# Layer 3's attention product by seven half-block products in a four-layer graph network on Trainium2

## The chip, the cores and the metric

The kernel runs on one core of one Trainium2 chip. The time is the device time in microseconds (us) of one execution, and the median over several executions is given. The core's engines are TensorE (PE in the profile, with PEld for its weight loads), VectorE (DVE), ScalarE (ACT), GpSimd (POOL) and the queue of SyncE (SP), which issues most DMAs.

## The reference

The input is 32 independent graphs of 512 nodes with 256 fp32 features each (`x`), and an integer adjacency matrix per graph (`adj`). Four attention layers follow one another, each with a layer norm and a ReLU ahead of it and a residual sum behind it. Layer 3, cut to what matters:

```
h   = relu(layernorm(x))
k   = h @ W
e   = leaky_relu((k @ a_1)^T + k @ a_2 + (k @ a_12) @ k^T)
e   = where(adj > 0, e, -9e15)
out = x + elu(h @ W_1 + (softmax(e) @ h) @ W_2)
```

## The kernel before

**Tiling.** A graph's 512 nodes are four tiles of 128 partitions (`NT` = 4); its 256 features are two halves of 128 (`HC` = 2, `HALF` = 128). Everything is fp32 on TensorE. A graph is a list of some hundred operations, made by `graph(b, ...)`, for each of `B` = 32 graphs. In each layer: layer norm (`normed`: statistics L558 on VectorE, the power L564 on GpSimd, the offset L567 on VectorE, the scaling L571 on ScalarE), a transposition by DMA (L576, L579, L591), values `v` = h times a weight (`scored_values`, matmuls at L809), scores, mask, exponential, the attention product (`attend`, L758), and the layer's end.

**Products by halves.** A product of two 2x2 block matrices takes eight block products, or seven if sums of blocks are formed ahead (Strassen's scheme in Winograd's form). The helper `seven` (L617) does the latter: the seven block products are written one after the other into two PSUM banks, `p` and `q`; between them ScalarE or VectorE copies or adds a result out (`write`, `add`), so that each product can accumulate onto what stands in the bank. The kernel before uses it for the features (L783), the values and `w3` (L809) and the scores (L874, L1042). `block_sums` (L649) forms the sums on VectorE. The attention product itself, in all four layers, is the plain one.

**Layer 3.** The scores come out transposed, keys on partitions, into two buffers `e3_0` and `e3_1` of two key tiles each. VectorE adds mask and bias (L1049, L1057), the row maximum is found by way of `crest3` (L1066 to L1085, two DMA transpositions), VectorE subtracts it (L1091), ScalarE takes the exponential of each buffer (L1094). `v3` holds h times W_2 in two halves of 128 columns, each with one more column; the last columns of a row are set to one, which lets the product give the sum of a row's weights. `w3` is h times W_1 less one. `attend(3, ...)` then multiplies: for two groups of two query tiles, for each of four key tiles, two matmuls of a 128x128 block of `e` with 259 columns of `v3`, into one bank for each query tile. The end of the layer, `fourth`, reads the bank: VectorE takes the reciprocal of the sum (L1123) and forms y = bank x reciprocal + `w3` (L1128). L1134, L1137 and L1140 form the elu and the residual, and a DMA on GpSimd's queue stores the graph (L1157).

**The order of work.** The class `Plan` orders the operations of all graphs. Each has an engine, a cost pair (how long it holds its engine, and when its result is there), operations that it comes after, and the buffers that it uses. `Plan.order` walks through a modelled time: on each engine the ready operation with the earliest due time goes next, if its buffers are free. Due times come from the last operation backward, with a spacing between graphs; `Plan.best` tries 64 pairs of spacings and keeps the order whose replay ends first. Each engine then executes its instructions in that order. Six graphs can be in flight (`FLIGHT`); the large buffers are 34 pages of 4 KB per partition (`PAGES`), PSUM has 8 banks, and there are 5 buffers for `v`.

Of the kernel before, what the change touches and what calls it, by code (L numbers as in the profile page):

```python
# [11 lines left out]
F32 = mybir.dt.float32  # L12
# [4 lines left out]
ALU = mybir.AluOpType  # L17
PSUM = bass.MemoryType.PSUM

P = 128  # L20
# [13 lines left out]
def pe(n512=0, n258=0, n256=0, nt=0):  # L34
    t = n512 * PE512 + n258 * PE258 + n256 * PE256 + nt * PET
    return t, t + 170.0
# [3 lines left out]
V_MASK, V_CODE, V_HALF, V_PSUM, V_ADD = (602.0, 683.0), (600.0, 690.0), (600.0, 690.0), (395.0, 484.0), (334.0, 425.0)  # L40
A_COPY, A_HALF, A_PRELU, A_EXP, A_TANH = (477.0, 597.0), (253.0, 373.0), (570.0, 693.0), (519.0, 640.0), (373.0, 474.0)
A_BIAS, A_PRELU2 = (570.0, 687.0), (629.0, 722.0)
G_POW, G_STORE = (800.0, 850.0), (900.0, 900.0)
V_SUM, V_BLOCK, V_FULL = (334.0, 425.0), (790.0, 880.0), (1140.0, 1225.0)
A_EXP_TWO, A_PRELU_TWO = (960.0, 1070.0), (1050.0, 1160.0)
A_HALF_BIAS = (345.0, 460.0)
# [161 lines left out]
def kernel(  # L208
# [31 lines left out]
    nc = tc.nc  # L240
    B, N, H = x.shape
    NT = N // P
    HC = H // P
    HALF = H // 2
# [4 lines left out]
    LEAD = 2  # L249

    const = ctx.enter_context(tc.tile_pool(name="const", bufs=1))
    work = ctx.enter_context(tc.tile_pool(name="work", bufs=1))
# [4 lines left out]
    cols, pair, stat, turned = [P, HC, N], [P, NT, H], [P, NT], [P, NT, N]  # L257
# [4 lines left out]
        "hT": (cols, F32, "page"), "fa": (cols, F32, "page"), "zT": (cols, F32, "page"), "row": (cols, F32, "page"),  # L262
        "xn": (pair, F32, "page"), "y": (pair, F32, "page"), "z": (pair, F32, "page"), "r": (pair, F32, "page"),
        "w": (pair, F32, "page"), "crest": ([P, 4, N], BF16, "page"),
        "hs": ([P, 4, N // 2], F32, "page"), "fs": ([P, 4, N // 2], F32, "page"),
        "code": (turned, BF16, "code"), "adj": (turned, I32, "adj"),
        "planes": ([P, 2, H], U16, "planes"), "planesT": ([P, 2 * HC, P], U16, "planesT"),
# [158 lines left out]
    for n, dst, w, key in (("w0", w0_s, w0, "raw9"), ("att", att_s, att_w, "raw10")):  # L426
# [11 lines left out]
    a = [load(l1_sb, rows_of(l1_w), "raw0")]  # L438
    t = transposed(l1_sb, lambda: halves(l1_wide()), a, "raw0", "raw11")
# [4 lines left out]
    a = [load(lambda i=i: halves(l2_wide())[:, :, i, :], rows_of(l2_w)[:, :, i * HALF : (i + 1) * HALF], "raw12")  # L444
         for i in range(2)]
    t = transposed(lambda: halves(l2_wide()), l2_wt, a, "raw1", "raw12")
    a = t + [load_column(l2_ac, l2_a.rearrange("o n -> (o n)"))]
    a = a + product(lambda d: l2_wide()[:, d, :: HALF + 1], l2_wt,
                    lambda c: l2_ac.rearrange("p (o c) -> p c o", o=2)[:, c, :], 2, a, "raw1", "raw12")
    ready["l2"] = seven_of(l2_wide, l2_aug, HALF + 1, a, "raw12")  # L450

    t = transposed(l3_sb, wt3, [load(l3_sb, rows_of(l3_w), "raw2")], "raw2", "raw4")
    a = product(lambda d: awt()[:, d, :], a12_sb, lambda c: wt3()[:, c, :], H,
                t + [load(a12_sb, rows_of(l3_a12), "raw3")], "raw3", "raw4", "raw5")
    a = product(lambda d: m3_sb()[:, d, :], wt3, lambda c: awt()[:, c, :], H, a, "raw4", "raw5", "raw6")
# [4 lines left out]
    a = [load(lambda i=i: l3_wide()[:, :, i * (HALF + 1) : i * (HALF + 1) + HALF],  # L460
              rows_of(l3_w2)[:, :, i * HALF : (i + 1) * HALF], "raw8") for i in range(2)]
# [8 lines left out]
    for i in range(VALUES):  # L470
        v = const.tile([P, NT, LEAD + H + 1], F32, tag=f"v{i}", name=f"v{i}")
# [4 lines left out]
    def graph(b, adj_before, x_before):  # L476


        T = Tiles(b)

        def op(engine, cost, after, emit, *keys, size=0, weights=()):
            return plan.op(engine, cost, after, emit, b, T.uses(keys) + W.uses(weights), size)

        def two(g):
            return slice(2 * g, 2 * g + 2)

        def half(i):
            return slice(i * N // 2, (i + 1) * N // 2)
# [45 lines left out]
        for g in range(NT // 2):  # L534
            code = op("V", V_CODE, [got_adj[2 * g + 2], code], partial(classes, g), "adj", "code", "slot")
            for t in (2 * g, 2 * g + 1):
                if b:
                    coded.append(op("D", D_TURN, [code], partial(turn_code, t), "code", "codeT"))
                else:
                    key = f"bank_c{t}"  # L540
                    a = op("PE", pe(nt=NT), [code], partial(turn_code_pe, t, key), "code", key)
# [75 lines left out]
        def seven(key, cost, after, keys, work, write, add, beside=0):  # L617

            p, q = f"bank_{key}p", f"bank_{key}{'p' if beside else 'q'}"

            def times(x, bank, start, fresh, *wait):
                return op("PE", cost, after(x) + list(wait), lambda: work(x, T[bank][:, start:], fresh), bank, *keys)

            c11 = write(0, 0, p, 0, [times(1, p, 0, True)])
            two = times(2, q, beside, not beside, c11)
            c12 = write(0, 1, p, 0, [times(6, p, 0, False, c11)])
            c22 = write(1, 1, p, 0, [times(7, p, 0, False, c12)])  # L640
            four = times(4, p, 0, False, c22)
            c21 = write(1, 0, p, 0, [four])
            c11 = add(0, 0, q, beside, [two, c11])

            c22 = add(1, 1, q, beside, [times(5, q, beside, True, four, c11), c22])
            c12 = add(0, 1, q, beside, [times(3, q, beside, False, c22), c12])
            return {(0, 0): c11, (0, 1): c12, (1, 0): c21, (1, 1): c22}
# [100 lines left out]
        def attend(l, es, vs, use):  # L748


            done, a = [], None
            lead = (LEAD, 1, 1, 0)[l]
            for ts in parts(l):
                keys = [f"bank_a{l}{t}" for t in ts]

                def product(ts, c, keys):
                    for t, key in zip(ts, keys):
                        nc.tensor.matmul(T[key][:, : LEAD + H + 1 - lead], e(l, c)[:, t * P : (t + 1) * P],  # L758
                                         T[f"v{l}"][:, c, lead:], start=(c == 0), stop=(c == NT - 1))

                for c in range(NT):
                    a = op("PE", pe(n258=2 * len(ts)), [es[c], vs[c], a], partial(product, ts, c, keys),
                           *keys, f"v{l}", f"e{l}_{c // 2}")
                done += [use(t, a, key) for t, key in zip(ts, keys)]
            return done

        def product_of(key):

# [45 lines left out]
        if b == 0:  # L814

            qs, vs, es = [], [], []
            for k in range(HC):
                key = f"bank_f0{k}"
# [6 lines left out]
                a = op("PE", pe(n512=4), hs + ready["raw10"], partial(features, k, key), key, "hT0", weights=["raw10"])  # L825
                qs.append(op("A", A_COPY, [a], lambda k=k, key=key: nc.scalar.copy(T["fa0"][:, k, :], T[key]), key, "fa0"))
            for t in range(NT):
                key = f"bank_v0{t}"
# [6 lines left out]
                a = op("PE", pe(n256=4), [hs[t]] + ready["raw9"], partial(values, t, key), key, "hT0", weights=["raw9"])  # L835
                vs.append(op("V", V_ADD, [a], lambda t=t, key=key: nc.vector.tensor_add(
                    T["v0"][:, t, LEAD : LEAD + H], T[key][:, :H], b0_sb), key, "v0"))
            for c in range(NT):
                key = f"bank_q0{c}"

                def similar(c, key):
# [4 lines left out]
                a = op("PE", pe(n512=4), qs, partial(similar, c, key), key, "hT0", "fa0")  # L846
                a = op("A", A_COPY, [a], lambda c=c, key=key: nc.scalar.activation(
                    e(0, c), T[key], AF.Exp, scale=float(H) ** -0.5), key, f"e0_{c // 2}")
                es.append(op("V", V_MASK, [a, m0], lambda c=c: nc.vector.tensor_tensor(
                    e(0, c), e(0, c), T["mask0"][:, c, :], ALU.mult), "mask0", f"e0_{c // 2}"))  # L850
        else:
            right_after, right = block_sums("hs0", "hT0", lambda j, l, T=T: T["hT0"][:, j, half(l)], hs, left=False)
# [10 lines left out]
            def add_v0(i, l, key, start, after):  # L863
# [3 lines left out]
            vs = seven("v0", pe(nt=4), lambda x, after=right_after: after(x) + ready["w0"], ("hT0", "hs0"),  # L867
                       partial(by_nodes, w0_s, right), write_v0, add_v0, beside=N // 2)
            vs = [tuple(vs.values())] * NT
            left_after, left = block_sums("fs0", "fa0", lambda i, j: T["fa0"][:, j, half(i)], qs, left=True)  # L870
# [27 lines left out]
            es = {}  # L898
# [3 lines left out]
            es = [(es[0, c // 2], es[1, c // 2]) for c in range(NT)]  # L902
# [21 lines left out]
        a = None  # L924
        for c in range(NT):
            a = op("PE", pe(n512=4), [ys[c], a], partial(again, c), "bank_z0", "bank_z1", "y0", f"e0_{c // 2}")
        zs = [op("A", A_COPY, [a], partial(evacuate_z, k), f"bank_z{k}", "zT") for k in range(HC)]
        xs = []
        for g in range(NT // 2):
            key = f"bank_o{g}"  # L930
# [18 lines left out]
            a = op("PE", pe(n256=8), zs + ready["w1"], partial(second_conv, g, key), key, "zT")  # L949
            bs = [op("V", V_PSUM, [a] + ready["b1"], partial(biased, 2 * g + j, key), key, "z0") for j in range(2)]  # L950
            a = op("A", A_EXP, bs, partial(tanh2, g), "z0")
# [7 lines left out]
        right_after, right = block_sums("hs1", "hT1", lambda j, l: T["hT1"][:, j, half(l)], hs, left=False)  # L959
        vb = scored_values(1, right_after, right, l1_aug, ready["l1"])  # L960
        vs = [tuple(vb.values())] * NT
        es = leaky_exp_t(1, vs, 1.0)
        es = [op("V", V_FULL, [es[g]], partial(masked1, g), "codeT", f"e1_{g}") for g in (0, 1)]
        es = [es[c // 2] for c in range(NT)]
# [16 lines left out]
        right_after, right = block_sums("hs2", "hT2", lambda j, l: T["hT2"][:, j, half(l)], hs, left=False)  # L981
        vb = scored_values(2, right_after, right, l2_aug, ready["l2"])
        vs = [tuple(vb.values())] * NT
        es = leaky_exp_t(2, vs, -1.0)
# [4 lines left out]
        es = [op("V", V_FULL, [es[g]], partial(masked2, g), "codeT", f"e2_{g}") for g in (0, 1)]  # L989
        es = [es[c // 2] for c in range(NT)]  # L990
# [26 lines left out]
        us, xs = attend(2, es, vs, third), []  # L1017
        for g in range(NT // 2):
            a = op("V", V_MASK, [u[0] for u in us[two(g)]], partial(add_lower, g), "y2", "x")
# [122 lines left out]
        def store_part(ts):  # L1142
            nc.sync.dma_start(out=out[b].rearrange("(t p) h -> p t h", p=P)[:, ts, :], in_=T["y3"][:, ts, :])

        us = attend(3, es, vs, fourth)
        last = []
        for ts in parts(3):
            ts = slice(ts[0], ts[-1] + 1)
# [55 lines left out]
```

## Time and profile before

| what | value |
|---|---|
| median of 3 executions | 2356.08 us (2354.88 to 2357.17) |
| profiled execution | 2353.99 us |
| its span, first to last instruction | 2351.9 us |
| granted TensorE clock | 1.00 |
| PE, PEld busy | 2327.6, 1991.7 us |
| DVE, ACT, POOL busy | 2000.2, 1687.7, 263.5 us |

The span is the profiled execution seen from its first instruction to its last; the 2.1 us beside it are start and end. Busy time is the time in which an engine has at least one instruction under way. A matmul's shown duration overlaps with the next one's, so what a matmul costs is read from start to start. Each fp32 matmul of the source stands in the profile as two MATMUL records, each with a weight load of its own.

### The profile page before, as it was taken

The numbers are of one execution on the slowest core, as the hardware profiler recorded it, in microseconds if no ns is written. First come the engines' busy times: TensorE is split into PE (matmuls) and PEld (weight loads), VectorE is DVE, ScalarE is ACT, GpSimd is POOL, SyncE is SP. The second block draws the span as 40 slices with busy tenths as digits, with TensorE's granted clock in tenths as the row PEclk, the third lists the DMA queues.
The fourth block names the chain that finished last, engine by engine and source line by source line (L and its number), as shares of the span: only waits on it lengthen the run. The fifth ranks groups of instructions, "written<-read, shape, count | busy, mean of one in ns | idle before, by whom it ended". The sixth has DMA issues, their size and how long they took to land.

```text
span 2351.9 us, 36467 instructions
## 1 busy us (share of the span) xinstructions
PE 2327.6 (99%) x12374; PEld 1991.7 (85%) x12374; DVE 2000.2 (85%) x5100; ACT 1687.7 (72%) x3165; POOL 263.5 (11%) x316
## 2 busy tenths in 40 slices
PE   7999999999999999999999999999999999999998
PEld 5888888888888898888888888988888888888887
DVE  6878788888888898888988888988889888887898
ACT  5567677767787767786767876777867677766884
POOL 3000111010111110110111111101111011010110
PEclk9999999999999999999999999999999999999999
DMA  7431233422333423334323343323342333421321
GB/s 197 90 77 39 52 84 77 92 61 73 92 68 86 91 49 86 79 75 94 84 55 83 73 86 72 90 62 70 88 93 57 78 92 62 90 55 25 59 52 41
DMA packets 429850, 178.18 MB, mean 76 GB/s; under 512 B 384128, under 2 KB 401664, under 8 KB 429664
## 3 DMA queue, kind: packets, MB, share of 16 engines
q1 hardware_dynamic: 424288, 157.51, 31.3%
q0 software_dynamic: 5232, 18.23, 2.4%
q8 instruction: 97, 1.59, 0.3%
q14 instruction: 89, 0.73, 0.1%
q10 hardware_dynamic: 144, 0.13, 0.0%
HBM read 67.64 MB, written 16.89 MB: 36 GB/s over the span
## 4 chain that ended last, share of the span: by engine, by line
PE 94%; DVE 3%; ACT 2%; DMA 1%; issue 0%; SPq 0%; DVEq 0%; ACTq 0%
PE bank_a L758 36%; PE bank_z L918 9%; PE bank_o L936 5%; PE bank_s3p L1042 5%; PE bank_q0p L874 4%; PE bank_f3p L783 4%; PE bank_v0p L809 4%; PE bank_f0p L783 4%; PE bank_w3p L809 4%; PE bank_q0q L874 3%; PE bank_s3q L1042 3%; PE bank_v1p L809 2%; PE bank_v2p L809 2%; PE bank_v3p L809 2%; PE bank_v1q L809 2%; PE bank_v3q L809 2%
## 5 line engine op out<-in xcount | busy, mean ns | idle before, releaser
L758 PE MATMUL bank_a<-v,e 128*128 128x258 f32 (+2 forms) x4096 | 1027.2, 381 | 3.0 <-DVE e L956 2.2
L758 PEld LDWEIGHTS bank_a<-v,e 128*128 128x128 f32 x4096 | 736.3, 190 | 108.9 <-issue 23.2
L591 ACT COPY hT<-planesT 128x512 uint16<-128x512 uint16 x508 | 383.2, 768 | 182.1 <-DMA planesT<-planes 170.7
L564 POOL TENSOR_TENSOR rstd<-ve,mhalf 128x2 f32<-128x2 f32 x256 | 227.9, 899 | 1896.9 <-DVE ve L561 1684.2
L571 ACT ACTIVATE xn<-x,off,rstd 128x256 f32<-128x256 f32 x512 | 284.8, 597 | 115.5 <-DVE off L567 115.2
L918 PE MATMUL bank_z<-e,y 128*128 128x512 f32 x512 | 240.8, 592 | 0.6 <-ACT y L909 0.6
L576 DVE COPY planes<-xn 128x512 uint16<-128x512 uint16 x380 | 155.9, 419 | 41.1 <-DMA planesT<-planes 28.3
L558 DVE BATCH_NORM_STATS2 st<-x 128x6 f32<-128x512 f32 x256 | 175.7, 695 | 5.0 <-DMA x<-in_x_dram 4.8
L732 ACT ACTIVATE e<-row,v 128x512 f32<-128x512 f32 x224 | 153.9, 721 | 0.0
L918 PEld LDWEIGHTS bank_z<-e,y 128*128 128x128 f32 x512 | 92.8, 190 | 66.2 <-issue 59.8
L735 ACT ACTIVATE e<-e 128x1024 f32<-128x1024 f32 x128 | 135.9, 1062 | 0.1
L936 PE MATMUL bank_o<-w_sb,zT 128*128 128x256 f32 x512 | 120.3, 379 | 0.0
L1049 DVE SCALAR_TENSOR_TENSOR e<-bank_s3p,v,mask 128x256 f32<-128x256 f32 x256 | 111.4, 476 | 10.2 <-PE bank_s3p L1042 9.1
L936 PEld LDWEIGHTS bank_o<-w_sb,zT 128*128 128x128 f32 x512 | 96.9, 190 | 13.0
L667 DVE TENSOR_TENSOR hs<-hT 128x512 f32<-128x512 f32 x127 | 86.7, 683 | 24.2 <-ACT hT L591 24.1
L664 DVE TENSOR_TENSOR hs<-hT,hs 128x256 f32<-128x256 f32 x254 | 105.8, 417 | 1.5
L1091 DVE TENSOR_TENSOR e<-e,crest 128x1024 f32<-128x1024 f32 x64 | 78.0, 1220 | 32.3 <-ACT crest L1085 32.3
L956 DVE SCALAR_TENSOR_TENSOR e<-codeT,e 128x1024 f32<-128x1024 bf16 x64 | 78.1, 1220 | 30.8 <-ACT e L735 30.6
L885 DVE TENSOR_TENSOR e<-bank_q0p,mask 128x512 f32<-128x512 f32 x124 | 84.7, 683 | 16.5 <-PE bank_q0p L874 15.9
L882 ACT ACTIVATE e<-e 128x512 f32<-128x512 f32 x124 | 77.9, 630 | 28.6 <-DVE e L893 25.0
L940 DVE SCALAR_TENSOR_TENSOR z<-bank_o,rs,b_sb 128x256 f32<-128x256 f32 x128 | 56.9, 479 | 41.1 <-PE bank_o L936 40.4
L695 ACT COPY v<-bank_v2p 128x258 f32<-128x258 f32 x128 | 47.9, 374 | 58.2 <-PE bank_v2p L809 57.4
(201 smaller groups left out, 4799.8 us busy)
## 6 DMA issues: line engine op xcount, KB each, us to landing
adj<-in_adj_dram SPq DMA_DIRECT2D x128, 256.0 KB
x<-in_x_dram SPq DMA_DIRECT2D x31, 512.0 KB
out_dram<-y POOLq DMA_DIRECT2D x31, 512.0 KB, 3.7
row<-row SPq DMA_DIRECT2D x56, 256.0 KB
planesT<-planes SPq DMA_TRANSPOSE x508
codeT<-code SPq DMA_TRANSPOSE x124
crest<-crest SPq DMA_TRANSPOSE x64
row<-sT SPq DMA_DIRECT2D x56, 2.0 KB
```

The costliest lines, as they stand in the source:

```text
L558: nc.vector.bn_stats(T[f"st{l}"][:, g, :], T["x"][:, two(g), :].rearrange("p t h -> p h t"))
L564: nc.gpsimd.tensor_tensor(T[f"rstd{l}"][:, two(g)], T[f"ve{l}"][:, two(g)], mhalf[:, two(g)], ALU.pow)
L571: nc.scalar.activation(T[f"xn{l}"][:, t, :], T["x"][:, t, :], AF.Relu, bias=T[f"off{l}"][:, t : t + 1], scale=T[f"rstd{l}"][:, t : t + 1])
L576: (nc.scalar.copy if l in BYACT else nc.vector.tensor_copy)(T[f"planes{l}_{t}"], bits)
L591: nc.scalar.copy(bits[:, :, :, t * P : (t + 1) * P], T[f"planesT{l}_{t}"].rearrange("p (b c) n -> p b c n", b=2))
L758: nc.tensor.matmul(T[key][:, : LEAD + H + 1 - lead], e(l, c)[:, t * P : (t + 1) * P], T[f"v{l}"][:, c, lead:], start=(c == 0), stop=(c == ...
L783: nc.tensor.matmul(p[:, : N // 2], w[:, x - 1, :], right(x), start=fresh, stop=True, skip_group_check=True)
L809: nc.tensor.matmul(p[:, j * k : (j + 1) * k], right(x)[:, j * P : (j + 1) * P], w[:, x - 1, :], start=fresh and j == 0, stop=True, skip_gr ...
L874: nc.tensor.matmul(p[:, j * N // 2 : (j + 1) * N // 2], right(x)[:, j * P : (j + 1) * P], left(x), start=fresh and j == 0, stop=True, skip ...
L918: nc.tensor.matmul(T[f"bank_z{k}"], T["y0"][:, c, k * P : (k + 1) * P], e(0, c), start=(c == 0), stop=(c == NT - 1))
L936: nc.tensor.matmul(T[key][:, j * H : (j + 1) * H], T["zT"][:, k, t * P : (t + 1) * P], w1_sb[:, k, :], start=(k == 0), stop=(k == HC - 1))
L1042: nc.tensor.matmul(p[:, j * N // 2 : (j + 1) * N // 2], left(x)[:, j * P : (j + 1) * P], right(x), start=fresh and j == 0, stop=True, skip ...
```

## The change

For graphs 0 to 26, layer 3's attention product is done by `seven`; the last five graphs keep `attend`. The new function `attend_by_seven` forms four sums of blocks of `v3` (`one_and_three`, which makes two at once, `two_` and `four_`) and four sums of blocks of the weights `e` (`weights_one` to `weights_four`) on VectorE. Three of these stand in new pages (`es3_0`, `es3_1`, `vs3`), `two_` and `weights_two` overwrite blocks of `v3` and `e3_0`. One GpSimd memset (`edge`) writes the columns that carry row sums in one of the sums. Each of the seven products is four matmuls of a 128x128 block with 128 columns, or 130 in products 3 and 5. ScalarE copies four results from PSUM to `y3` and VectorE adds three onto it; two of the adds come with a reciprocal of two columns. `both_terms_of` then forms y from `y3` in SBUF where `both_terms` read PSUM. `seven` itself now takes its list of buffers for each product.

```diff
+V_SUM_TWO, G_EDGE = (480.0, 570.0), (120.0, 150.0)
...
+        "es": ([P, 2, 2, N // 2], F32, "page"), "vs": ([P, 2 * N], F32, "page"),
...
-                return op("PE", cost, after(x) + list(wait), lambda: work(x, T[bank][:, start:], fresh), bank, *keys)
+                return op("PE", cost, after(x) + list(wait), lambda: work(x, T[bank][:, start:], fresh), bank,
+                          *(keys(x) if callable(keys) else keys))
...
+        def attend_by_seven(l, es, vs, start):
+            WIDE = HALF + 2
+            v, low, high, far, near = f"v{l}", f"e{l}_0", f"e{l}_1", f"es{l}_0", f"es{l}_1"
...
+            def edge():
+                nc.gpsimd.memset(pair()[:, 0, :, HALF:], -1.0)
+
+            def one_and_three():
...
+                nc.vector.tensor_tensor(pair()[:, :, :, :HALF], diagonal,
+                                        value(0, 1).unsqueeze(1).to_broadcast([P, 2, 2, HALF]), ALU.subtract)
+
+            def two_():
+                nc.vector.scalar_tensor_tensor(value(0, 1), pair()[:, 0, :, :HALF], -1.0, value(1, 1), ALU.mult, ALU.subtract)
+
+            def four_():
+                nc.vector.scalar_tensor_tensor(fourth_sum(), value(0, 1), -1.0, value(1, 0), ALU.mult, ALU.subtract)
...
+            def weights_one():
+                nc.vector.tensor_tensor(T[far][:, 0], weight(1, 0), weight(1, 1), ALU.add)
+
+            def weights_three():
+                nc.vector.tensor_tensor(T[far][:, 1], weight(0, 0), weight(1, 0), ALU.add)
+
+            def weights_two():
+                nc.vector.tensor_tensor(weight(1, 0), weight(0, 0), T[far][:, 0], ALU.add)
+
+            def weights_four():
+                nc.vector.tensor_tensor(T[near][:, 0], weight(0, 1), weight(1, 0), ALU.add)
+
+            e_ = op("G", G_EDGE, start, edge, f"vs{l}")
+            v1 = v3 = op("V", V_MASK, vs + start, one_and_three, v, f"vs{l}")
+            v2 = op("V", V_SUM, [v1], two_, v, f"vs{l}")
+            v4 = op("V", V_SUM, [v2], four_, v, f"vs{l}")
+            w1 = op("V", V_MASK, es, weights_one, low, high, far)
+            w3 = op("V", V_MASK, [w1], weights_three, low, far)
+            w2 = op("V", V_MASK, [w3], weights_two, low, far)
+            w4 = op("V", V_MASK, [w2], weights_four, low, high, near)
+            after = {1: es[:1] + vs, 2: es[1:] + vs, 3: [w4] + vs, 4: es[1:] + [v4], 5: [w1, v1, e_], 6: [w2, v2], 7: [w3, v3]}
...
+            def work(x, p, fresh):
+                a, b_ = left[x](), right[x]()
+                k = b_.shape[2]
+                for i in range(2):
+                    for j in range(2):
+                        nc.tensor.matmul(p[:, i * WIDE : i * WIDE + k], a[:, j, i * P : (i + 1) * P], b_[:, j, :],
+                                         start=fresh and i == j == 0, stop=True, skip_group_check=True)
...
+            def write(i, f, key, start, after):
+                return op("A", A_HALF, after, lambda: nc.scalar.copy(block(i, f), part(key, start)[:, :, :HALF]), key, f"y{l}")
+
+            def add(i, f, key, start, after):
+                def emit():
+                    nc.vector.tensor_tensor(block(i, f), block(i, f), part(key, start)[:, :, :HALF], ALU.add)
+                    if f == 1:
+                        nc.vector.reciprocal(T[f"rs{l}"][:, two(i)], part(key, start)[:, :, WIDE - 1])
+
+                return op("V", V_SUM_TWO if f else V_SUM, after, emit, key, f"y{l}")
+
+            done = seven(f"a{l}", pe(nt=8), lambda x: after[x], keys_of, work, write, add)
+            return [[done[i, 0], done[i, 1]] for i in (0, 0, 1, 1)]
...
-        us = attend(3, es, vs, fourth)
+        def both_terms_of(t):
+            y = T["y3"][:, t, :]
+            nc.vector.scalar_tensor_tensor(y, y, T["rs3"][:, t : t + 1], T["w3"][:, t, :], ALU.mult, ALU.add)
+
+        if b < B - 5:
+            cs = attend_by_seven(3, [es[0], es[2]], list(vs[0]), [row])
+            us = [op("V", V_PSUM, c + [wb[0, t // 2], wb[1, t // 2]], partial(both_terms_of, t), "y3", "w3")
+                  for t, c in enumerate(cs)]
+        else:
+            us = attend(3, es, vs, fourth)
```

More of the change, by code (lines that the diff above doesn't have):

```diff
@@ L765, in attend, with keys_of, value, pair @@
             return done
+        def attend_by_seven(l, es, vs, start):
+            WIDE = HALF + 2
+            v, low, high, far, near = f"v{l}", f"e{l}_0", f"e{l}_1", f"es{l}_0", f"es{l}_1"
+            def keys_of(x):
+                return {1: [low], 2: [high], 3: [near], 4: [high, f"vs{l}"], 5: [far, f"vs{l}"], 6: [low], 7: [far, f"vs{l}"]}[x] + [v]
+            def value(j, f, k=HALF):
+                return T[v][:, two(j), f * (HALF + 1) : f * (HALF + 1) + k]
+            def pair():
+                return T[f"vs{l}"][:, : 4 * WIDE].rearrange("p (x j k) -> p x j k", x=2, j=2)
+            def fourth_sum():
+                return T[f"vs{l}"][:, 4 * WIDE : 4 * WIDE + 2 * HALF].rearrange("p (j k) -> p j k", j=2)
+            def edge():
+                nc.gpsimd.memset(pair()[:, 0, :, HALF:], -1.0)
+            def one_and_three():
+                w = T[v]
+                line = LEAD + H + 1
+                diagonal = bass.AP(tensor=w.tensor, offset=w.offset,
+                                   ap=[list(w.ap[0]), [2 * line + HALF + 1, 2], [line, 2], [1, HALF]])
+                nc.vector.tensor_tensor(pair()[:, :, :, :HALF], diagonal,
[4 more added lines that the diff above has]
+                nc.vector.scalar_tensor_tensor(fourth_sum(), value(0, 1), -1.0, value(1, 0), ALU.mult, ALU.subtract)
+            def weight(i, j):
+                return T[(low, high)[j]][:, :, half(i)]
+            def weights_one():
[15 more added lines that the diff above has]
+            after = {1: es[:1] + vs, 2: es[1:] + vs, 3: [w4] + vs, 4: es[1:] + [v4], 5: [w1, v1, e_], 6: [w2, v2], 7: [w3, v3]}
+            left = {1: lambda: weight(0, 0), 2: lambda: weight(0, 1), 3: lambda: T[near][:, 0], 4: lambda: weight(1, 1),
+                    5: lambda: T[far][:, 0], 6: lambda: weight(1, 0), 7: lambda: T[far][:, 1]}
+            right = {1: lambda: value(0, 0), 2: lambda: value(1, 0), 3: lambda: value(1, 1, WIDE), 4: fourth_sum,
+                     5: lambda: pair()[:, 0], 6: lambda: value(0, 1), 7: lambda: pair()[:, 1, :, :HALF]}
+            def work(x, p, fresh):
[5 more added lines that the diff above has]
+                                         start=fresh and i == j == 0, stop=True, skip_group_check=True)
+            def block(i, f):
+                return T[f"y{l}"][:, two(i), f * HALF : (f + 1) * HALF]
+            def part(key, start):
+                return T[key][:, start : start + 2 * WIDE].rearrange("p (i k) -> p i k", i=2)
+            def write(i, f, key, start, after):
[8 more added lines that the diff above has]
+            return [[done[i, 0], done[i, 1]] for i in (0, 0, 1, 1)]
```

## The prediction

> **What bounds the kernel now.** I read the page first, from the busy shares down to the chain, and then asked the trace for groups by shape, waits, windows and the timeline. First the shares and the slices of the page:
>
> ```profile
> span 2351.9 us, 36467 instructions
> ...
> PE 2327.6 (99%) x12374; PEld 1991.7 (85%) x12374; DVE 2000.2 (85%) x5100; ACT 1687.7 (72%) x3165; POOL 263.5 (11%) x316
> ...
> PE   7999999999999999999999999999999999999998
> PEld 5888888888888898888888888988888888888887
> DVE  6878788888888898888988888988889888887898
> ...
> PE 94%; DVE 3%; ACT 2%; DMA 1%; issue 0%; SPq 0%; DVEq 0%; ACTq 0%
> ```
>
> TensorE is full in every slice but the ends, and the chain that ended last is 94% matmuls. A busy PE need not be one at its peak, so two more views: the waits of PE between 216 and 2093 us, whose only row is the first line below, and windows of one graph each. A graph has about 12374 / 32 = 387 matmul records, and the windows of 72.2 us hold 386 to 389, so the steady period is 72.2 us.
>
> ```profile
> PE bank_a L758 <- DVE e L956: 1.7, 1, 1.7
> ```
>
> ```profile
> 600.00:672.20 72.20, 72.20 (x386) 61.87 (x385) 62.18 (x160) 52.70 (x101) 8.36 (x9) 1.00 0.40 89
> 672.20:744.40 72.20, 72.20 (x386) 62.00 (x385) 62.91 (x159) 53.84 (x102) 7.74 (x9) 1.00 0.29 66
> ```
>
> The columns are length, then PE, PEld, DVE, ACT and POOL busy, the clock, the DMA share and GB/s. In 1877 us PE waited 1.7 us for anyone; the clock is full; DVE is busy 62.5 us of 72.2 and idle 10. So time taken from PE shortens the run one for one, as long as DVE, the next engine, keeps up.
>
> Is PE at its peak rate? The groups by shape and the timeline answer:
>
> ```profile
> L758 PE MATMUL bank_a<-v,e 128*128 128x259 f32 x1024 | 263.5, 382 | 0.3 <-ACT e L1094 0.3
> ...
> L809 PE MATMUL bank_w3p<-l_w1s,hs 128*128 128x128 f32 x512 | 77.8, 274 | 0.0
> ```
>
> ```profile
> 1200.92 0.61 PE L809 MATMUL bank_v3p<-l_aug,hs 128*128 128x129 f32 x4
> 1201.37 0.61 PE L809 MATMUL bank_w3p<-l_w1s,hT 128*128 128x128 f32 x4
> 1201.81 0.60 PE L783 MATMUL bank_f0p<-hT,att_s 128*128 128x256 f32 x2
> ...
> 1203.56 4.53 PE L758 MATMUL bank_a<-v,e 128*128 128x259 f32 x20
> 1207.92 1.02 PE L874 MATMUL bank_q0p<-fa,hT 128*128 128x256 f32 x4
> ```
>
> The durations (382 and 274 ns) overlap; the cost is from start to start. Twenty records of 259 columns take 1207.92 - 1203.56 = 4.36 us, 218 ns each; four of 128 columns 0.44 us, 110 ns; four of 129, 0.45 us, 113 ns. Half the columns at half the time: narrow products lose nearly nothing here. The count shows that each matmul of the source stands as two records (16 in layer 3's attention of a graph, 1024 / 32 = 32 records).
>
> [...]
>
> **The change part by part**, for each of 27 graphs (b < 27; the last five run as before).
>
> Removed on PE: 32 records of 259 columns, 32 x 218 = 6.98 us. Added: seven products of four matmuls, 28, so 56 records; product 3 and product 5 carry two columns more (sums of rows), so 40 x 110 + 16 x 113 = 6.21 us. **Saved: 0.77 us a graph, 20.8 us in all.** It lies wholly on the path. Weight loads go from 32 to 56 a graph, 27 x 24 = 648 more records in each PE row; the L809 streams show that they hide.
>
> Added on DVE, from these rows and starts:
>
> ```profile
> L667 DVE TENSOR_TENSOR hs<-hT 128x512 f32<-128x512 f32 x127 | 86.7, 683 | 24.2 <-ACT hT L591 24.1
> L664 DVE TENSOR_TENSOR hs<-hT,hs 128x256 f32<-128x256 f32 x254 | 105.8, 417 | 1.5
> ```
>
> ```profile
> 1201.86 0.41 DVE L664 TENSOR_TENSOR fs<-fa,fs 128x256 f32<-128x256 f32 x1
> 1202.18 0.41 DVE L1115 TENSOR_TENSOR w<-w,bank_w3p 128x256 f32<-128x256 f32 x1
> 1202.51 0.41 DVE L798 TENSOR_TENSOR fa<-fa,bank_f0p 128x256 f32<-128x256 f32 x1
> ```
>
> 256 elements hold DVE 0.33 us, and 512 hold it 0.60. The new one_and_three and the four weight sums are 5 x 0.60 = 3.00; two_ and four_ 0.66; three adds from PSUM 0.99; two reciprocals against four, 2 x 0.08 less; both_terms_of reads SBUF in place of PSUM, 0.33 for 0.39 (L1128, two in 0.87 us), 4 x 0.06 less. Net **+4.1 us a graph**. Against the old idle time of 10 us and the shorter period of 71.4 us DVE rises from 62.5 to 66.6, 93%. I cost it at nearly nothing because PE hides it, and if DVE falls behind the cover is gone. The same view in stretches of 12 us:
>
> ```profile
> 1212.00:1224.00 12.00, 12.00 (x67) 10.79 (x66) 11.77 (x32) 4.18 (x8) 1.49 (x2) 1.00 0.37 104
> ...
> 1248.00:1260.00 12.00, 12.00 (x53) 9.07 (x52) 7.13 (x14) 10.95 (x20) 0.00 (x0) 1.00 0.55 130
> ```
>
> DVE at 98% for 12 us (the first line) costs PE nothing, since six graphs are in flight and others' matmuls stand ready; and in each period there is a stretch where DVE is at 59% and ACT at 91%.
>
> ACT gets four copies of 256 elements from PSUM, 0.37 us each as at L791, with 0.27 from start to start: +1.1 us on 53 of 72, hidden. POOL gets one memset of 128x2x2; the nearest row is a POOL memset of 128x4 at 101 ns: 0.1 us on an engine busy 8 of 72. It waits for the row of tops (L1085's ACT instruction) and for its page; behind it in POOL's queue stand the rstd powers of L564, for whom DVE (off, L567) and then ACT wait. With POOL idle nearly 90% I price it at nothing; from below nothing is excluded, since it removes no work, and its upper end is one power's 0.9 us on a graph, seldom. No DMA is added, removed or moved.
>
> New waits: weights_one waits for both exponentials of L1094 where a matmul waited for one, with other graphs' vector work behind it on DVE; product 6 waits for ACT's copy of product 1's bank, and so on through the chain, with other graphs' matmuls behind it on PE. The sums (4 x 0.60) and the copies lengthen layer 3's end by some 5 us. Six graphs at 72 us give each 433 us from start to end, so that is hidden while PE has others' work. Three more pages (es 2, vs 1) of 34 are held from the sums to the last products.
>
> No row of before shows what PE loses to these. Bounds: a gain of up to 4 us, if the newly planned order also fills the gaps that the drain has now (2093 to 2309 us: PE busy 212.8 of 216); a loss of up to the whole added DVE time. I take 0.1 us a graph, 2.7 us, some 5% of the added vector work showing through. Sum against the profiled execution: span 2351.9 - 20.8 + 2.7 = 2333.8, with the 2.1 us around it (2353.99 - 2351.9) 2335.9. The median is 2.1 above the profiled one: **2338**.
>
> **The rivals.**
> 1. Saving nearly whole, as summed: 2338 (own range 2332 to 2345). For it: PE's empty list of waits at DVE 98%. Chance 0.60.
> 2. DVE is tight: at 93% fewer matmuls stand ready, and PE loses 0.45 us a graph, 12 us: 2347 (2345 to 2354). For it: one full stretch of DVE will now meet the next. Chance 0.19.
> 3. **Slower: the added vector work reaches PE.** Place: the weight sums, which come in a burst right behind layer 3's exponentials, when DVE is needed to free score banks and to mask. It decides from 0.77 / 4.1 = 19% of the added DVE time onwards. At a third, 27 x (1.37 - 0.77) = +16: 2372. Against it: the light stretch and six graphs of freedom. Chance 0.13.
> 4. The change saves little of what it says: narrow products stall on their weight loads. At 122 ns a record 56 would cost 6.83 us and leave 0.15 a graph, or 4 us: 2352. The L809 rows at 110 to 113 speak against it. Chance 0.08.
>
> **How the numbers follow.** A measurement of this kernel can tell about 0.2%, 4.7 us: faster is below 2351.4, slower above 2360.8. Cases 1 and 2 give faster 0.78, case 4 with the edges of 2 and 3 gives 0.08 within, and the rest, 0.14, is slower. The range 2332 to 2357 holds the first two cases and the fourth, and leaves out most of the third.
>
> **What would show it.** In the profile after: PE still 99% or more in the middle slices, with some 13020 matmul records; the new products starting 110 to 113 ns apart; windows of 71.4 us per graph; DVE at about 91% of the span (2000 + 27 x 4.1 = 2111 us of 2334) and ACT at 74%; hardly a row of PE waiting. Wrong would be: PE rows that wait for weight sums, for v's sums or for ACT's copies adding up to over 10 us; slices where DVE stands at 9 while PE drops to 8; or a record spacing above 120 ns.

## The result and the profile after

The changed kernel takes **2349.04 us** (median of 7, 2346.27 to 2351.59), the kernel before 2356.08 (7 runs): ratio 0.9972, 95% interval 0.9962 to 0.9981. It is 7 us faster where 18 were forecast. The profiled execution took 2347.43 us, its span 2345.7.

The page of the kernel after, its spans, busy shares, two rows of slices and the chain:

```profile
span 2345.7 us, 38186 instructions
...
PE 2314.3 (99%) x13022; PEld 1999.0 (85%) x13022; DVE 2111.6 (90%) x5316; ACT 1704.1 (73%) x3273; POOL 268.6 (11%) x343
...
PE   7999999999999999999999999999999999999998
...
DVE  6878899999999999999999899998999999987898
...
PE 89%; ACT 6%; DVE 3%; DMA 2%; issue 1%; SPq 0%; ACTq 0%; DVEq 0%
```

PE's slices look as before, and DVE has what was added to it. The news is in the chain: ACT has 6% of it where it had 2%. The new products themselves are as cheap as forecast. From the groups by shape and the timeline of the kernel after:

```profile
L838 PE MATMUL bank_a3p<-v,e 128*128 128x128 f32 x432 | 57.1, 275 | 1.3 <-DVE e L814 1.3
L838 PE MATMUL bank_a3q<-vs,es 128*128 128x130 f32 x216 | 28.6, 275 | 0.0
```

```profile
1037.60 1.05 PE L838 MATMUL bank_a3p<-v,e 128*128 128x128 f32 x8
1038.49 0.60 PE L877 MATMUL bank_f3p<-hs,m 128*128 128x256 f32 x2
```

Eight records in 0.89 us are 111 ns each. PE's waits between 216 and 2093 us, one row of 1.7 us before, are now:

```profile
PE bank_f3p L877 <- ACT fa L887: 4.1, 6, 1.2
PE bank_a3p L838 <- DVE e L814: 1.3, 1, 1.3
PE bank_v1p L903 <- ACT v L698: 1.0, 1, 1.0
PE bank_z L1012 <- ACT y L1003: 0.9, 1, 0.9
PE bank_s3p L1136 <- DVE e L1143: 0.6, 1, 0.6
```

The longest row is none of the new products': it is another graph's feature product (`features_t`, L877), which waits for ScalarE to empty its bank. Only the second row is a wait of a new product (L838), once in 27 graphs.

Windows from 216 to 2093 us (length, PE busy and records, PEld, DVE, ACT, POOL, clock, DMA share, GB/s), first of before, then of after:

```profile
216.00:2093.00 1877.00, 1875.26 (x9994) 1613.23 (x9993) 1615.36 (x4104) 1368.70 (x2569) 208.51 (x235) 1.00 0.35 76
```

```profile
216.00:2093.00 1877.00, 1869.02 (x10661) 1626.36 (x10660) 1729.32 (x4334) 1387.70 (x2684) 213.25 (x262) 1.00 0.34 77
```

PE is idle 8.0 us of this stretch where it was idle 1.7. Since a matmul is shown up to 0.16 us longer than the time to the next one's start (275 ns against 111), busy time hides part of each gap. So I also summed over the trace, for each matmul record, the time to the next start less the usual one of its shape, and call what lies 30 ns or more above it **gaps**: in this stretch 2.2 us in 5 places before, 12.2 us in 37 after. The usual time of a shape is the mean over both traces without such outliers, 111.1 ns at 128 columns, 111.9 at 130 and 218.8 at 259. Over the whole run the usual times sum to 2317.8 us before and 2297.1 after, 20.7 less. The rest, gaps and small deviations together, grew by 14.8: 10.9 in the middle, 1.3 ahead of 216 us, 2.6 behind 2093. That leaves 5.9 of the 6.2 us between the spans (2351.9 and 2345.7).

So the work left PE as forecast, and most of it came back, for the most part as time in which PE's next instruction was not ready. One such place, on the timeline of the kernel after, PE first, then ACT:

```profile
1041.09 1.89 PE L1030 MATMUL bank_o<-w_sb,zT 128*128 128x256 f32 x8
1043.72 0.70 PE L877 MATMUL bank_f3p<-hT,m 128*128 128x256 f32 x2 [0.74 <-ACT fa L887]
1044.25 0.59 PE L877 MATMUL bank_f3p<-hs,m 128*128 128x256 f32 x2
```

```profile
1042.05 0.35 ACT L848 COPY y<-bank_a3p 128x256 f32<-128x256 f32 x1
1042.31 0.37 ACT L698 COPY v<-bank_v3p 128x258 f32<-128x258 f32 x1
1042.57 0.73 ACT L735 ACTIVATE e<-row,v 128x512 f32<-128x512 f32 x1
1043.20 0.47 ACT L887 ACTIVATE fa<-bank_f3p,l_u 128x256 f32<-128x256 f32 x1
```

ScalarE copies one of the new products (L848), then values, then works on another graph's layer (L735), and only then empties the bank that PE waits for. PE stands idle for 0.74 us until 1043.72. A product of the new kind (product 7) follows behind on PE at 1044.68, although it lacked nothing: its block sums had ended by 1033.17, and the copy that frees its bank (L848, above) at 1042.41.

### The profile page after: what moved, and what is told of

It reads as the page before. It is cut to its first block, busy times and chain, and to the rows that moved or that the text cites. A ratio compares the mean times of both kernels' runs of the same rounds, so it can differ in the third digit from the quotient of the medians.

```text
span 2345.7 us, 38186 instructions
## 1 busy us (share of the span) xinstructions
PE 2314.3 (99%) x13022; PEld 1999.0 (85%) x13022; DVE 2111.6 (90%) x5316; ACT 1704.1 (73%) x3273; POOL 268.6 (11%) x343
## 4 chain that ended last, share of the span: by engine, by line
PE 89%; ACT 6%; DVE 3%; DMA 2%; issue 1%; SPq 0%; ACTq 0%; DVEq 0%
PE bank_a L761 27%; PE bank_z L1012 7%; PE bank_s3p L1136 5%; PE bank_q0p L968 5%; PE bank_v0p L903 4%; PE bank_f0p L877 4%; PE bank_f3p L877 4%; PE bank_o L1030 4%; PE bank_w3p L903 4%; PE bank_a3p L838 4%; PE bank_q0q L968 3%; PE bank_s3q L1136 3%; PE bank_a3q L838 3%; PE bank_v1p L903 2%; PE bank_v3p L903 2%; PE bank_v2p L903 2%
## 5 line engine op out<-in xcount | busy, mean ns | idle before, releaser
L761 PE MATMUL bank_a<-v,e 128*128 128x258 f32 (+2 forms) x3232 | 819.3, 382 | 1.8 <-ACT e L1188 0.7
L761 PEld LDWEIGHTS bank_a<-v,e 128*128 128x128 f32 x3232 | 578.5, 191 | 78.8 <-issue 11.6
L573 ACT ACTIVATE xn<-x,off,rstd 128x256 f32<-128x256 f32 x512 | 279.4, 600 | 215.2 <-DVE off L569 214.8
L735 ACT ACTIVATE e<-row,v 128x512 f32<-128x512 f32 x224 | 159.0, 734 | 0.2 <-DMA row<-row 0.2
L667 DVE TENSOR_TENSOR hs<-hT,hs 128x256 f32<-128x256 f32 x254 | 106.1, 418 | 0.5
L1231 ACT ACTIVATE r<-y,one 128x512 f32<-128x512 f32 (+1 forms) x65 | 46.5, 715 | 56.2 <-DVE y L1241 47.9
```

What stands on the lines that cost most here:

```text
L573: nc.scalar.activation(T[f"xn{l}"][:, t, :], T["x"][:, t, :], AF.Relu, bias=T[f"off{l}"][:, t : t + 1], scale=T[f"rstd{l}"][:, t : t + 1])
```

## The experiments

The first theory, **A**: the added vector work costs PE its ready matmuls, either DVE's load as such (A-plain) or the products' wait for the sums (A-narrow). Its rival, **B**: the chain of seven products (product, copy by ScalarE, product in the same bank) leaves PE empty. Gaps are counted as above, from 216 to 2093 us, in the one profiled execution of each kernel. Each ratio is to executions of the kernel before that were timed beside the experiment.

**e1, no weight sums.**

```diff
-            w1 = op("V", V_MASK, es, weights_one, low, high, far)
...
-            w4 = op("V", V_MASK, [w2], weights_four, low, high, near)
+            w1 = w2 = w3 = w4 = tuple(es)
```

> The changed kernel without the four sums of weight blocks (the products take plain blocks of e, and y3 is multiplied by zero, so the output is not the reference's); the seven products, their chain through ScalarE and the pages stay. Theory A (the added vector work, 2.4 of 4.1 us a graph of it here, makes matmuls late): PE's gaps between 216 and 2093 us fall from some 12 us to under 4 and the time from 2349 to 2336 to 2340. Theory B (the chain product, ScalarE copy, product in two banks leaves PE empty): the gaps stay, 2346 to 2349.

2337.78 us, ratio 0.9922 (0.9909 to 0.9936); gaps 1.7 us. B falls: the whole chain of products, with its four copies on ScalarE, is there and leaves PE hardly any gaps. Without the sums the kernel takes the time that was forecast with them.

**e2, vector load without followers**, the kernel before with seven additions of 512 elements more in each of 27 graphs:

```diff
+            for i in range(7):
+                op("V", V_MASK, [es[0], es[2]], partial(load_vector, i), "e3_0", "e3_1", "es3_0")
```

> The kernel before with seven more vector instructions of 512 elements (4.2 us) in each of the first 27 graphs, behind layer 3's exponentials, for whose results nobody waits. Theory A in its plain form (DVE's load as such starves PE): PE gaps of some 10 us appear, 2363 to 2370. Theory A in its narrow form (only vector work that matmuls wait for costs) and theory B: within 2 us of before, 2355 to 2358.

2356.86 us, 1.0005 (0.9997 to 1.0013); gaps 0.6 us. The window of this kernel:

```profile
216.00:2093.00 1877.00, 1876.98 (x9999) 1614.60 (x9998) 1711.72 (x4291) 1377.00 (x2573) 205.94 (x235) 1.00 0.34 76
```

DVE is busy 1711.7 us, nearly as long as after the change, and PE is idle for 0.02. Load alone, where the plan may put it anywhere, is free.

**e3, seven products in every second graph, and e4, in three of four.**

```diff
-        if b < B - 5:
+        if b < B - 5 and b % 2 == 0:
```

> Seven products only in every second of the first 27 graphs (14 of them). If the loss belongs to each graph that has them (theory B, or narrow A without any slack): 14/27 of the 7 us, 2352 to 2353. If the loss grows out of proportion with DVE's load (theory A): most of 14 x 0.8 = 11 us is kept, 2345 to 2348, as fast as the changed kernel.

2347.23 us, 0.9966 (0.9953 to 0.9978); gaps 1.9 us with 14 graphs changed. In e4 the condition is `b < B - 5 and b % 4`:

> Seven products in three of four of the first 27 graphs (20 of them). Loss in proportion (B): 20/27 of 7 us, 2351. Loss out of proportion (A): 20 x 0.8 = 16 us less some 6, 2345 to 2347, a little faster than the changed kernel.

2346.11 us, 0.9959 (0.9946 to 0.9971); gaps 4.4 us with 20 graphs. Half the graphs bring as much as 27 do: the loss isn't a fixed price of each changed graph.

**e5, the sums made, but nobody waits.**

```diff
-                nc.vector.tensor_tensor(weight(1, 0), weight(0, 0), T[far][:, 0], ALU.add)
+                nc.vector.tensor_tensor(T[near][:, 1], weight(0, 0), T[far][:, 0], ALU.add)
...
+            w1 = w2 = w3 = w4 = tuple(es)
```

> The changed kernel with all four sums of weight blocks made in full, but into pages that no product reads (the products take plain blocks of e, and y3 is multiplied by zero, so the output is not the reference's). DVE does the same work as in the changed kernel. Theory A-narrow (the loss is the wait of the products for the sums): as with the sums left out, 2336 to 2340, PE gaps in the middle under 4 us. Theory A-plain (the loss is DVE's 93% at the shorter period): 2346 to 2350 with some 10 us of gaps, as the changed kernel.

2337.61 us, 0.9921 (0.9908 to 0.9933); gaps 2.3 us. Its window:

```profile
216.00:2093.00 1877.00, 1876.33 (x10703) 1634.45 (x10702) 1732.95 (x4355) 1398.42 (x2700) 190.17 (x263) 1.00 0.34 77
```

DVE is as busy as after the change (1733 against 1729 us) at the full saving on PE: A-plain falls as well. What remains is that products come behind the sums.

**e6, a shorter chain of sums.** In the changed kernel six of the eight sums stand in the three new pages; of the weight sums, the second alone overwrites a block of `e3_0` that the third one reads, so the order is first, third, second, and product 6 comes behind three sums. Here the second sum goes to the free half of `es3_1`:

```diff
-            w3 = op("V", V_MASK, [w1], weights_three, low, far)
-            w2 = op("V", V_MASK, [w3], weights_two, low, far)
+            w2 = op("V", V_MASK, [w1], weights_two, low, far, near)
+            w3 = op("V", V_MASK, es, weights_three, low, far)
```

> The changed kernel with the second sum written to the free half of page es3_1 in place of over a block of e3_0, so that it no longer comes behind the third: the chain ahead of product 6 is two sums long in place of three, and the fourth comes third. The same vector work, same output. A-narrow: PE gaps fall by more than half, 2336 to 2343. A-plain: no change, 2347 to 2350. If only the number of new orders tried matters (luck of the order), anything between.

**2338.45 us**, 0.9926 (0.9913 to 0.9940): 18 us faster than before, 11 faster than the change, with the same arithmetic. Gaps 5.2 us.

**e7, the new place, the old order**, against e6:

```diff
-            w2 = op("V", V_MASK, [w1], weights_two, low, far, near)
-            w3 = op("V", V_MASK, es, weights_three, low, far)
+            w3 = op("V", V_MASK, [w1], weights_three, low, far)
+            w2 = op("V", V_MASK, [w3], weights_two, low, far, near)
```

> As the short chain, with the second sum in the free half of es3_1, but again behind the third by a dependency in the plan alone: the place without the shorter chain. A-narrow and A-plain: as the changed kernel, 2346 to 2351, some 10 us of gaps. If it was the overwritten block of e3_0 that held PE (products and sums on one page), as the short chain.

2350.28 us, 0.9975 (0.9965 to 0.9985); gaps 18.4 us. The loss is back: it hangs on the second sum coming behind the third, not on the place. How that acts, e13 will show.

**e8, the third sum on GpSimd**, e6 with

```diff
-            w3 = op("V", V_MASK, es, weights_three, low, far)
+            w3 = op("G", (1500.0, 1600.0), es, weights_three, low, far)
```

> The short chain with the third sum on GpSimd (planned at 1.5 us), which only product 7 waits for: DVE has 0.6 us less a graph. A-narrow: no gain over the short chain, within 2 us of it. A-plain: a further gain of 2 us or more. If GpSimd needs far more than 1.5 us for 512 elements, or disturbs DVE, slower than the short chain.

2338.50 us, 0.9927 (0.9914 to 0.9939); gaps 5.0 us. There is no gain, but neither was DVE relieved, as the windows of e6 and then of e8 show:

```profile
216.00:2093.00 1877.00, 1874.14 (x10685) 1631.15 (x10685) 1733.21 (x4351) 1396.93 (x2697) 213.61 (x263) 1.00 0.34 77
216.00:2093.00 1877.00, 1874.92 (x10691) 1632.62 (x10690) 1731.54 (x4326) 1397.69 (x2697) 230.63 (x288) 1.00 0.34 77
```

DVE is busy 1731.5 us where it was busy 1733.2: other DVE instructions took 16.9 us longer beside the additions on GpSimd, and these took 16.2 off its hands (last section). So e8 says nothing about A-plain, which had already fallen with e5.

**e9 to e12, the same pair at other counts**, against the luck of a single order. e9 and e11 are the changed kernel with `b < B - 3` and `b < B - 8`, e10 and e12 the short chain with the same.

> The changed kernel's order of sums (third ahead of second), with plain products in the last three graphs in place of five, which makes another plan. If the long chain of sums is the cause: again some 10 us of PE gaps between 216 and 2093 us and 2345 to 2352. If it was the luck of one order: anything from 2335 to 2352.

> The short chain with plain products in the last three graphs. Cause is the chain: gaps under 5 us, 6 to 13 us faster than the long chain of the same count, 2335 to 2341. Luck of the order: no fixed sign against its partner.

> The changed kernel's order of sums with plain products in the last eight graphs (24 with seven products). Cause is the chain: gaps of 8 to 14 us, 2348 to 2353. Luck of the order: anything from 2339 to 2353.

> The short chain with plain products in the last eight graphs. Cause is the chain: gaps under 5 us and 2338 to 2344, 5 to 12 us faster than the long chain of the same count. Luck of the order: no fixed sign against its partner.

| plain graphs at the end | long chain | gaps | short chain | gaps |
|---|---|---|---|---|
| 3 | e9: 2354.84, 0.9997 (0.9990 to 1.0004) | 15.8 | e10: 2340.94, 0.9939 (0.9924 to 0.9954) | 5.1 |
| 5 | after: 2349.04, 0.9972 (0.9962 to 0.9981) | 12.2 | e6: 2338.45, 0.9926 (0.9913 to 0.9940) | 5.2 |
| 8 | e11: 2353.70, 0.9992 (0.9985 to 0.9999) | 8.9 | e12: 2346.10, 0.9957 (0.9940 to 0.9973) | 5.8 |

The sign is the same three times, by 14, 11 and 8 us. The long chains of e9 and e11 were slower than expected, and e12 too; the gaps of e10 and e12 are a little above the 5 us expected, and e10 leads by 14 us where 6 to 13 were. Part of this lies outside the middle: the deviations ahead of 216 us are 14.2 us in e11 and 14.5 in e12 (before 9.8), in both with a stretch at half the TensorE clock (last section), and behind 2093 us 15.6 in e9 (before 7.4). The ends of the run change with each plan, by some us that no theory here gave. In e7 and e9 one stretch at half clock falls into the middle and makes 1.7 us of the gaps there.

At this point I took it that product 6 came too late on the chip. The traces spoke against it: in the changed kernel product 6 starts a median 1.5 us after the second sum has ended. Hence two theories on how the chain acts, **C**: the engines take their instructions in a fixed order, and the plan made a worse one out of the longer chain; **D**: the sums are late on the chip. The plan alone can be told another length:

**e13, the changed kernel, planned as if the third sum were short.**

```diff
-            w3 = op("V", V_MASK, [w1], weights_three, low, far)
+            w3 = op("V", V_TINY, [w1], weights_three, low, far)
```

> The changed kernel, all its instructions and waits kept, but with the third sum entered in the plan as 0.08 us long in place of 0.60, so that the plan orders the engines as if the chain ahead of product 6 were short. Theory C (it is the fixed order made from the long chain): 2336 to 2343, gaps in the middle under 6 us. Theory D (the sums are late on the chip): 2346 to 2355, gaps of 10 us and more.

**2338.63 us**, 0.9928 (0.9915 to 0.9942); gaps 4.0 us.

**e14, the short chain, planned as if the second sum were late.**

```diff
-            w2 = op("V", V_MASK, [w1], weights_two, low, far, near)
+            w2 = op("V", (602.0, 1550.0), [w1], weights_two, low, far, near)
```

> The short chain, with the second sum's result entered in the plan 0.87 us later than it comes (1.55 for 0.68), so that the plan orders as if the chain were long. Theory C: part or all of the loss comes back, 2343 to 2352. Theory D: as the short chain, 2337 to 2341.

2345.43 us, 0.9958 (0.9945 to 0.9970); gaps 11.9 us. The windows and PE's waits (216 to 2093 us) of e13 and then of e14:

```profile
216.00:2093.00 1877.00, 1875.68 (x10702) 1634.20 (x10701) 1733.17 (x4355) 1400.81 (x2697) 194.20 (x263) 1.00 0.34 77
```

```profile
PE bank_v1q L903 <- DVE v L702: 0.7, 1, 0.7
PE bank_v1p L903 <- DVE hs L667: 0.4, 1, 0.4
PE bank_a L761 <- DVE e L1050: 0.2, 1, 0.2
```

```profile
216.00:2093.00 1877.00, 1869.94 (x10658) 1626.42 (x10657) 1728.06 (x4333) 1385.12 (x2680) 213.46 (x262) 1.00 0.35 77
```

```profile
PE bank_f3p L877 <- ACT fa L887: 5.5, 5, 2.3
PE bank_v1p L903 <- ACT v L698: 0.7, 1, 0.7
PE bank_a L761 <- DVE e L1050: 0.7, 2, 0.3
```

e13 has every instruction and every dependency of the changed kernel, in another order, and PE is idle 1.3 us in place of 8.0. e14 has the short chain's instructions and loses 7 us against it, with the row of L877 waiting for ScalarE back. **C holds, D falls.** The sums even come later in e13: from the end of the second exponential to the end of the second sum it is 4.1 us on average there, 3.7 in the changed kernel, and 2.9 in e14, which is slow. It is not the luck of one plan either: with 24 to 29 changed graphs, five plans made with the long chain (after, e7, e9, e11, e14) have gaps of 8.9 to 18.4 us, five made with the short one (e6, e8, e10, e12, e13) 4.0 to 5.8.

## Why the prediction was right and wrong

- **The saving on PE: right.** 0.77 us a graph and 20.8 in all were forecast; the usual times of the records fell by 20.7. The spacing is 111 ns at 128 columns, and the 13022 records were forecast as some 13020. Rival 4 (stalls on weight loads) did not come.
- **The work on DVE: right in sum.** 4.1 us a graph forecast, (2111.6 - 2000.2) / 27 = 4.1 measured. There is some luck in it: the terms as written add up to 4.25 (3.00 + 0.66 + 0.99 - 0.16 - 0.24), and one of them was off, since `both_terms_of` from SBUF was to be 0.06 us cheaper than from PSUM, but is shown at 478 ns where the old one took 475. The 0.60 us of 512 elements is the time to the next start (L667 at 1212.36 us in the kernel before, the next instruction at 1212.96); the new sum L811 held DVE as long, 0.61 us (1032.48 to 1033.09). ACT is at 73% where 74 was forecast.
- **What PE loses: the step that failed.** I set 0.1 us a graph, 2.7 in all, reasoning that with six graphs in flight others' matmuls stand ready. The measured term is 14.8 us. The error was in "stand ready": PE takes its instructions in the order in which the plan wrote them. In the trace of the changed kernel all 13022 matmul records stand in that order, and product 7, ready at 1042.41, stood behind the waiting feature product until 1044.68, with PE idle for 0.74 us in between. There a matmul that waited held up a ready one, and e13 against the changed kernel shows what an order is worth here: 10 us. With e13's order the same term is 3.6 us, close to the 2.7. The prediction treated the new order as a possible gain of 4 us and not as a possible loss.
- **The rivals.** In size the result is near rival 2 (2347, "DVE is tight"), but its mechanism is not what happened: e5 has the same DVE load and none of the loss. Rival 3 (the sums reach PE) named the right place, the sums behind the exponentials, and a wrong way: the products seldom wait for them (1.3 us in one place), and it is their length in the plan that counts. My signs of failure named PE rows that "wait for weight sums, for v's sums or for ACT's copies", over 10 us in sum; all rows together show 7.9, most of it for other work of ACT, while the gaps that busy time partly hides are 12.2.
- **The size without the bad order: right.** 2338 was forecast; e13, the same instructions in another order, takes 2338.63, and its span of 2335.9 stands against the 2333.8 of the sum. Of those 2.1 us, 0.9 are the term above (3.6 for 2.7) and 1.4 a first matmul that starts later (9.98 us for 8.54).

**What stays open.** That the order costs the 10 us is shown; which of its features does is not. The plan orders all engines at once, so the runs don't tell PE's order from ScalarE's or VectorE's. Kernels with large gaps share the row of L877 waiting for ScalarE, and their orders switch more from graph to graph: product 2 runs ahead of product 6 in 9 to 15 of 24 to 29 changed graphs (after, e7, e9, e11, e14), in 7 to 9 in e6, e10 and e12, and in one or two in e1, e3, e4, e5, e8 and e13. But most of the gaps lie in the graphs with product 6 first (9.4 of the 12.2 us in the changed kernel), and no run tried this switching by itself. Nor did any run separate what the ends of the run owe to the order.

## What to carry to other kernels

Where instructions stand in an order made ahead of time, a change of the work also makes a new order, and here that order was worth half of the saving; so a small gain (or loss) should be judged over several orders, by telling the planner slightly other costs as e13 does, before the work itself is blamed. To tell load from order, add the same load where nobody waits for it (e2), and make the same results without using them (e5). And a buffer reused in place ties two operations that have nothing else to do with each other: writing the second sum elsewhere (e6) cost no time, and by way of the plan it brought 11 us.

## What the runs showed of the hardware

In the kernel after, TensorE's granted clock fell to half twice while matmuls ran, for 3.41 us each time, from 36.19 and from 2200.24 us. Both falls came behind gaps on PE, which in the 3.41 us ahead of them was shown busy for 1.39 and 1.61 us. Two windows around them:

```profile
36.50:40.00 3.50, 3.50 (x12) 2.95 (x11) 2.34 (x12) 2.98 (x7) 3.38 (x6) 0.56 0.55 78
2200.50:2204.00 3.50, 3.50 (x13) 3.01 (x13) 3.50 (x6) 2.41 (x6) 0.65 (x1) 0.55 0.19 37
```

PE shows as fully busy in both, at a mean clock of 0.56 and 0.55. In the second fall four records of 258 columns took 1.85 us from start to start (2200.67 to 2202.52), and 0.87 us behind it (2204.84 to 2205.71). By my estimate each fall costs half of its length (3.41 x 0.5), some 1.7 us, together 3.4 of the 14.8, and most of what the two ends lost. It is no peculiarity of the change: the profiled execution of the kernel before, at a mean clock of 1.00, has such a fall only behind its last matmul, but every other trace (mean clocks 0.997 to 0.999) has one that begins between 32 and 37 us, that of e2 with its plain products too (0.997), and 19 of the 39 executions of the kernel before beside e9 to e12 have a mean clock of 0.998, which I estimate at 7 us or more at half clock (0.0015 x 2350 x 2). What brings a fall about, the runs do not show.

A GpSimd addition of 128x512 fp32 took 1.56 us in e8, where VectorE's took 0.68 in e6, and VectorE got slower beside it:

```profile
L811 POOL TENSOR_TENSOR es<-e 128x512 f32<-128x512 f32 x27 | 42.2, 1562 | 209.7 <-ACT e L1188 200.7 <-issue 9.0
```

In e8, 25 VectorE instructions took 0.3 us or more above the median of their kind, 16.9 us in all, and each of them began within a GpSimd addition. In e6, without these additions, there is none. A subtraction of 512 elements from SBUF (L795) took up to 1.77 us for 0.67, a mask of 16-bit values (L1122) 1.78 for 0.69, while additions of 258 elements with an operand in PSUM (L702) took 0.42 us within a GpSimd addition and 0.41 elsewhere. The 27 sums taken from VectorE are worth 27 x 0.60 = 16.2 us, as much as it lost.
